# The order of four long neighbour lists, and a group that begins with its first two tiles

## The chip, the cores and the metric

The kernel runs on one core of a Trainium2 chip. The metric is the device time of one execution in microseconds (us). It is given as the median of three executions. Engines are called as in the profile: PE is TensorE, DVE is VectorE, ACT is ScalarE, POOL is GpSimd, SP is SyncE.

## What is computed

Sixteen graphs of 1024 nodes with 64 channels go through two layers. The second layer is the costly one. For every node it takes the list of its neighbours, drops a few of them by rank (dilation), and aggregates each channel by three interpolated quantiles over what is left. The essential lines of the reference are:

```python
# layer 0
h = jnp.maximum(_layernorm(x, axis=-1), 0.0)
x = x + matmul(adj / clip(sum(adj, axis=2), 1.0, None), h)
# layer 1
h = jnp.maximum(_layernorm(x, axis=-1), 0.0)
nb = (adj_ > 0) & (~eye)[None]
m = nb.sum(-1); rank = jnp.cumsum(nb, axis=-1) - 1
skip = jnp.where(m > 10, (m + 1) // 2, 1)
removed = nb & (skip > 1) & mask & ((rank + 1) % skip == 0)
rem = removed | swapaxes(removed, 1, 2)
adj_d = jnp.where(rem, 0.0, adj_)
agg = sum of wt * quantile(h of the neighbours in adj_d, tau) for tau in 0.25, 0.5, 0.75
x = x + (relu((h + agg) @ W1 + b1) @ W2 + b2) * mask
```

The adjacency is sparse and uneven: the first nodes of each graph have many neighbours, the later ones few. So most nodes have a short list, and a few have a long one.

## The kernel before, in words

The work has two stages, each of which is an ordered stream of instructions that a planner writes out while the kernel is built.

In the **first stage** (the pool `lay0`, line 1328) the batches are loaded one after another. Layer 0 is computed with transposes and products on PE. Each node's neighbours are listed as sorted keys with `max` operations on DVE. Every node's record (channels, the result of layer 0, 32 keys, its number and its mask) is scattered by POOL to `srt`, sorted by length of list. Four batches form a group, so there are four groups, and each has a table `tab` in DRAM with the rows that neighbours are gathered from. After a group is complete, its short lists are worked off; those of the groups 0 to 2 lie mostly within this stage. The last group (number 3) and the long lists come in the **second stage** (the pool `long`, line 1337).

`group` (line 1102) begins a group. It loads the records of all 32 tiles of 128 nodes (`recs`, one DMA of 544 KB). It then computes node numbers, gathers the full adjacency rows of the first tile (`gat_rows`), counts the neighbours of all tiles, and sorts the keys of tiles 1 to 31 (`keys`, with `max`, and `match_replace` where a list is longer than eight). It works out which neighbours are removed, in tile 1 from its keys and in tile 0 from the full row. It writes two dropped numbers per node into the table (`tab<-drop`, POOL), and copies the table to `whole` (SP). Then it adds one `Job` for each class of equal length.

`long_lists` (line 1239) treats the first tile's nodes of all groups together: four tiles of 128 nodes with at most 88, 31, 24 and 20 neighbours (`LONG`, line 40). For each list it loads the records (`lS`), gathers the adjacency rows (`lat`), finds the largest keys by segments, and makes the indices `lidx`. Then it adds a `Job` whose gathers write `lplaces0` (list 88, one buffer) or `lplaces` (the others, two buffers).

A `Job` (line 831) gathers one row per neighbour with one POOL instruction each (`run`, line 840). When all have landed, it marks removed neighbours (`rem`, `gone`, `ok`, `valid`, `q`, `wu` on DVE). ACT adds the marks to each gathered row. A sorting network of min and max on DVE follows, between `places` and `other` for short lists and between `lplaces` and `long_other` for long ones; there is one `long_other` and one set of `lgone` and `lwu`. ACT then scales the rows with the weights `w` or `lw` (128x67 for list 88), PE sums them with an identity matrix, and a small MLP (`layers`, line 1039) with ACT and PE follows. DVE adds the residual into `y`, and POOL scatters `y` to the output (`out_dram<-y`). `y` has six buffers.

The order of all instructions on an engine is fixed when the kernel is built, by the class `Plan` (line 234). Every stream names the engine of its next step and the earliest time for it. `Plan.run` (line 323) takes the step with the earliest time; among equal times the lower rank goes first. `Plan.note` (line 271) holds the cost model for each operation. The chip's engines then run their instructions strictly in that order, each waiting on semaphores for what it needs. The ranks that matter here are: -2000 for a group, -1500 for the preparation of long lists, -600 plus the number of the list for gathers of long lists, 100 times the group plus the class for short lists, 400 plus the number for the rest of long lists. DVE steps of a job get 900 less while fewer than 16 gathers are outstanding (`AHEAD`, line 214) and 2000 more otherwise. Outputs and MLP steps of short lists get -1000 and 5000 in the same two cases.

Nearly all instructions carry line 228, that of the helper which records them for the planner, so the profile is read by tile names.

Of the kernel before, what the change touches and what calls it, by code (L numbers as in the profile page):

```python
# [18 lines left out]
P = 128  # L19
# [9 lines left out]
NSEG = 4  # L29
# [204 lines left out]
class Plan:  # L234
# [4 lines left out]
    def __init__(self, nc):  # L239
        names = {"vector": "DVE", "scalar": "ACT", "tensor": "PE", "gpsimd": "POOL", "sync": "SP"}  # L240
        self.nc = SimpleNamespace(
            **{attr: Timed(self, name, getattr(nc, attr)) for attr, name in names.items()}
        )
        self.clock = dict.fromkeys([*names.values(), "DMA"], 0.0)
        self.ready, self.used, self.users = {}, {}, {}
        self.slots, self.streams = {}, []
        self.last = self.own = None
        self.parts = set()

    def tile(self, pool, shape, dtype, name, bufs, users=0):  # L250

# [16 lines left out]
    def at(self, *tiles):  # L268
        return max(self.ready.get(t.tensor.name, INF) for t in tiles)

    def note(self, engine, op, args, kwargs):
# [22 lines left out]
        elif engine == "PE":  # L294
            time = 0.1 + math.prod(out.shape[1:]) * 0.88e-3
            if op == "matmul" and rest[0].dtype == F32:
                time *= 2
        elif engine == "POOL":
            time, after = (1.27, 2.2) if op == "indirect_dma_start" else (0.15, 0.1)
            self.last = None  # L300
        else:
            start = max(start, self.clock["DMA"])
            busy = math.prod(out.shape) * 4 / 165e3

            time, after = 0.05, 2.2 + busy * (1 if 4 * out.shape[-1] >= 512 else 2)
            self.clock["DMA"] = start + busy
# [67 lines left out]
def list_path(ctx, tc, x, adj, nodemask, w1, b1, w2, b2, out, go):  # L374
# [727 lines left out]
    def group(g, kept=grp, name=""):  # L1102
# [16 lines left out]
        lists = recs[:, :, :8 * NSEG]  # L1119
        node = recs[:, :, REC - 2]  # L1120
        mask = recs[:, :, REC - 1]
        nodes = new(grp, [P, NTAU], F32, "nodes", 1)
        nc.vector.tensor_scalar(
            nodes, node, noff[:, s:s + 1], float(FIRST[g] * N), op0=OP.add, op1=OP.add
        )
        nodes_i = new(kept, [P, NTAU], I32, name + "nodes_i", 1 if name else 2)
        nc.vector.tensor_copy(nodes_i, nodes)
        progress["begun"] = g + 1
        yield "POOL", lambda: at(nodes_i)
        full = new(grp, [P, N], F32, "gat_rows", 1)  # L1130
        gather(full, adj_rows, nodes_i[:, 0:1])
        yield "DVE", always

        found = new(grp, [P, N], BF, "gfound", 1)[:, :NTAU * 8 * NSEG]
        found = found.rearrange("p (t e) -> p t e", t=NTAU)
        nc.vector.tensor_scalar(found, lists, 0.0, None, op0=OP.is_gt)
        m = tiny.tile([P, NTAU], F32, name="gm")
        nc.vector.tensor_reduce(m, found, AX.X, OP.add)
        over = tiny.tile([P, NTAU], F32, name="over")
        nc.vector.tensor_reduce(  # L1140
            over, found.rearrange("p t (s e) -> p t s e", e=8)[:, :, :, 7], AX.X, OP.max
        )
        nc.vector.memset(over[0 if four else HP:, 0:1], 0.0)
        big = tiny.tile([P, NTAU], F32, name="big")
        nc.vector.tensor_tensor(big, m, caps_sb, OP.is_gt)
        nc.vector.tensor_tensor(over, over, big, OP.max)
        nc.vector.tensor_reduce(ovf[:, g:g + 1], over, AX.X, OP.max)
# [5 lines left out]
        nc.vector.tensor_scalar(based, base, float(N), None, op0=OP.add)  # L1153

        drop = new(tiny, [P, 2, 2], F32, "drop", 2)
# [3 lines left out]
        for t in range(begin, NTAU):  # L1159
            nc.vector.max(out=keys[:, t, :8], in_=lists[:, t, :])  # L1160
            if caps[t] > 8:
                nc.vector.match_replace(
                    out=left, in_to_replace=keys[:, t, :8], in_values=lists[:, t, :],
                    imm_value=0.0,
                )
                nc.vector.max(out=keys[:, t, 8:], in_=left)
            if t % 8 == 0:
                yield "DVE", always

        assert all(cap <= T_THRESH for cap in caps[begin + 1:])  # L1170
        fst = slice(begin, begin + 1)
        skip = dilation(m[:, fst], mask[:, fst], 1)
        hit = tiny.tile([P, 2, 16], F32, name="hit")
        for e in range(2):
            nc.vector.tensor_scalar(
                hit[:, e, :], place1[:, :16], skip[:, e, :], None, op0=OP.is_equal
            )
            nc.vector.tensor_tensor(hit[:, e, :], hit[:, e, :], keys[:, begin, :], OP.mult)
        if four:
            nc.vector.tensor_reduce(drop[:, 1, :], hit, AX.X, OP.add)  # L1180
            nc.vector.tensor_scalar(
                drop[:, 1, :], drop[:, 1, :], -1.0, float(N), op0=OP.mult, op1=OP.add
            )
        for e in range(2):
            nc.vector.tensor_tensor(
                keys[:, begin, :], keys[:, begin, :], hit[:, e, :], OP.subtract
            )
        didx = new(tiny, [P, 2], I32, "didx", 2)
        index_of(didx, node[:, 0:2], float(PW), basep)
        idx = new(kept, [P, NTAU, 16], I32, name + "idx", 1 if name else 2)  # L1190
        index_of(idx, keys, -1.0, based)

        yield "DVE", lambda: at(full)
        nc.vector.scalar_tensor_tensor(
# [6 lines left out]
        skip = dilation(cum[:, N - 1:N], mask[:, 0:1], 1)  # L1201
# [6 lines left out]
        for e in range(2 if four else 1):  # L1208
# [8 lines left out]
                tc.declare_no_dep(ins.ins, other, reason="rows of their own")  # L1217
            other = ins.ins
        dropped = at(table)
        yield "SP", lambda: dropped  # L1220
        nc.sync.dma_start(whole[FIRST[g] * TS:R * TS, :], table)
        classes = []
# [16 lines left out]
    def long_lists(pool):  # L1239
# [1 line left out]
        yield "DVE", always  # L1241
        rev = new(pool, [P, N], HF, "rev", 1)
        nc.vector.tensor_scalar(rev, col_f, -1.0, float(N), op0=OP.mult, op1=OP.add)
        for l, K in enumerate(LONG):
            n = K + 1
            yield "SP", always
            S = new(pool, [P, 1, RW], F32, "lS", 4)
# [62 lines left out]
            for e in range(2):  # L1310
# [17 lines left out]
    with tc.tile_pool(name="lay0", bufs=2) as pool:  # L1328

        for stream, first in (  # L1330
# [303 lines left out]
```

## Time and profile before

| | us |
|---|---|
| median of three executions | 1513.86 |
| lowest, highest | 1511.95, 1516.6 |
| the profiled execution | 1512.82 |
| its span, first to last instruction | 1511.0 |

| engine | busy us | share of the span |
|---|---|---|
| DVE | 1191.3 | 79% |
| POOL | 957.2 | 63% |
| ACT | 816.4 | 54% |
| PE | 738.8 | 49% |

The span is divided by the stages at about 890 us. Before that point DVE is busy for 727 us of 890, and after it for 464 us. DMA moves 133 MB over the span, 88 GB/s on the mean; the two busy queues take 20.8% and 11.2% of the 16 engines' time.

A row of the timeline gives start, duration, engine, line, operation, output and inputs, and in brackets how long the engine had been idle and what ended that. A row of waits gives who waited for whom, total us, number of times and the longest. A row of busy times by stretch gives start and end, length, then busy us and count of instructions for PE, PE weight loads, DVE, ACT and POOL, then the granted PE clock, the busy share of the DMA engines and GB/s.

### The profile page before, as it was taken

How to read it: one execution, taken by the hardware profiler on the slowest of the kernel's cores; microseconds unless marked ns; L12 is line 12 of the kernel's file. 1: busy time of each engine (PE TensorE's matmuls, PEld its weight loads, DVE VectorE, ACT ScalarE, POOL GpSimd, SP SyncE). 2: the span in 40 equal slices, each digit the busy share in tenths (PEclk: the TensorE clock that was granted, in tenths of full speed). 3: DMA queues.
4: the chain of work that ended last, by engine and by line, in shares of the span. 5: the costliest groups of instructions: out<-in, count | busy, mean ns of one | idle time of the engine just before them, and what ended most of it. 6: DMA issues, size and time to landing. Idle time of an engine off the chain costs nothing. (4 is left out here: it accounts for less than half of the span.)

```text
span 1511.0 us, 15983 instructions
## 1 busy us (share of the span) xinstructions
PE 738.8 (49%) x3192; PEld 464.7 (31%) x3192; DVE 1191.3 (79%) x4104; ACT 816.4 (54%) x2789; POOL 957.2 (63%) x1154
## 2 busy tenths in 40 slices
PE   4778777327877556567667620024000123228542
PEld 2434334214544233343444320012000122216432
DVE  6777798997899779859869869893059999986875
ACT  7989878557879457757975520201050223148341
POOL 0122227777678757757777787667777777765083
PEclk8889888658888777869688755555555565558765
DMA  5445665424355253355341242111111111211010
GB/s 177 150 142 168 163 210 160 123 73 114 101 162 152 59 174 94 99 126 161 94 140 31 60 101 68 50 37 28 30 26 23 28 28 40 44 33 22 2 25 13
DMA packets 135718, 133.36 MB, mean 88 GB/s; under 512 B 100756, under 2 KB 103444, under 8 KB 135492
## 3 DMA queue, kind: packets, MB, share of 16 engines
q1 hardware_dynamic: 102876, 90.79, 20.8%
q0 software_dynamic: 32736, 41.47, 11.2%
q14 instruction: 78, 0.64, 0.1%
q8 instruction: 28, 0.46, 0.1%
HBM read 112.90 MB, written 23.61 MB: 90 GB/s over the span
## 5 line engine op out<-in xcount | busy, mean ns | idle before, releaser
L228 POOL DMA_INDIRECT places<-tab,idx x372 | 370.2, 995 | 131.7 <-issue 101.8
L228 PE MATMUL pt<-ident,prod 128*128 128x128 f32 (+1 forms) x736 | 160.2, 377 | 517.8 <-DVE prod L228 241.2
L228 PEld LDWEIGHTS pt<-ident,prod 128*128 128x128 f32 (+1 forms) x736 | 129.3, 256 | 550.4 <-ACT prod L228 412.4
L228 PE MATMUL ps_small<-att,h 128*65 128x512 f32 x512 | 254.7, 644 | 27.3 <-ACT h L228 10.5
L228 POOL DMA_INDIRECT srt<-row,to x128 | 125.9, 984 | 165.8 <-ACT row L228 144.0
L228 PE MATMUL pt<-ident,at 128*128 128x128 f32 x1024 | 176.7, 320 | 96.0 <-ACT att L228 71.1
L228 POOL DMA_INDIRECT lplaces<-whole,lidx x163 | 167.2, 1026 | 55.6 <-issue 48.5
L228 DVE MAX8 rec<-sg 128x8 f16<-128x256 f16 x512 | 180.1, 414 | 4.4
L228 PEld LDWEIGHTS pt<-ident,at 128*128 128x128 f32 x1024 | 136.9, 164 | 143.5 <-ACT att L228 93.8
L228 ACT ACTIVATE sg<-at 128x1024 f16<-128x1024 f32 x128 | 134.8, 1054 | 75.0 <-DMA at<-in_adj_dram 65.7
L228 ACT COPY att<-pt 128x512 f32<-128x512 f32 x256 | 141.9, 582 | 20.7 <-PE pt L228 18.8
L228 POOL DMA_INDIRECT places<-tab,last_idx x124 | 123.8, 998 | 41.3 <-issue 35.0
L228 PEld LDWEIGHTS ps_small<-att,h 128*65 128x65 f32 x512 | 74.7, 151 | 161.9 <-issue 123.2
L228 ACT ACTIVATE places<-places,gone 128x64 f32<-128x64 f32 x496 | 123.5, 335 | 0.5
L228 ACT ACTIVATE prod<-places,w 128x64 f32<-128x64 f32 x213 | 54.1, 336 | 120.5 <-DVE w L228 120.5
L228 POOL DMA_INDIRECT out_dram<-y,nodes_i x93 | 91.8, 987 | 22.6 <-issue 15.1
L228 DVE TENSOR_TENSOR sg<-sg,keyed 128x1024 f16<-128x1024 f16 x128 | 87.2, 681 | 23.7 <-ACT sg L228 23.7
L228 ACT ACTIVATE gone<-gone 128x15 f32<-128x15 f32 (+9 forms) x40 | 8.2, 206 | 169.2 <-DVE ok L228 169.0
L228 DVE TENSOR_TENSOR long_other<-lplaces 128x512 f32<-128x512 f32 (+5 forms) x124 | 64.1, 555 | 29.1 <-ACT lplaces L228 28.9
L228 DVE TENSOR_TENSOR other<-places,other 128x64 f32<-128x64 f32 (+6 forms) x204 | 69.6, 341 | 5.9
L228 PE MATMUL ps_small<-ot,w_sb 128*128 128x128 f32 (+3 forms) x112 | 47.6, 513 | 44.2 <-DVE y L228 31.2
L228 DVE TENSOR_TENSOR places<-places,other 128x64 f32<-128x64 f32 (+2 forms) x208 | 62.3, 309 | 4.9
(231 smaller groups left out, 1670.8 us busy)
## 6 DMA issues: line engine op xcount, KB each, us to landing
at<-in_adj_dram SPq DMA_DIRECT2D x128, 512.0 KB
places<-tab,idx POOLq DMA_INDIRECT x372, 2.5
whole<-tab SPq DMA_DIRECT2D x4, 1057.0 KB
tab<-row SPq DMA_DIRECT2D x16, 264.0 KB
xt<-in_x_dram SPq DMA_DIRECT2D x16, 256.0 KB
lplaces<-whole,lidx POOLq DMA_INDIRECT x163, 2.4
srt<-row,to POOLq DMA_INDIRECT x128, 2.7
places<-tab,last_idx POOLq DMA_INDIRECT x124, 2.4
```

Source lines behind the costliest of these rows:

```text
L228: ins = getattr(self._engine, op)(*args, **kwargs)
```

## The change

Three things change.

The long lists are prepared, gathered and ranked in the order 31, 24, 88, 20 instead of 88, 31, 24, 20. Buffers, capacities and the place of each list's nodes stay with the list.

A group loads the records of its first two tiles apart (`ahead`), ahead of the load of all records, which stays. From `ahead` it makes the row numbers of tile 0 (`row0`), gathers the adjacency rows, sorts the keys of tile 1, and computes and scatters the dropped nodes of both tiles. Only then does it wait for `recs`, sort the keys of tiles 2 to 31, make the indices, node numbers and counts, and copy the table. Each tile's keys 8 to 15 are set to zero one by one where the list is not longer than eight, instead of one memset of all keys.

In the second stage the planner takes PE's operations to be 1.5 times as long as before (`pace`). In the first stage it keeps 1.0.

```diff
+        self.pace = 1.0
...
+            time *= self.pace
...
+        ahead = new(kept, [P, 2, REC], F32, name + "ahead", 1 if name else 2)
+        nc.sync.dma_start(ahead, tiles[:, :2, R0:])
         nc.sync.dma_start(recs, tiles[:, :, R0:])
-        yield "DVE", lambda: at(recs)
+        yield "DVE", lambda: at(ahead) + 1.0
+        node = ahead[:, :, REC - 2]
+        nodes = new(grp, [P, NTAU], F32, "nodes", 1)
+        row0 = new(tiny, [P, 1], I32, "row0", 2)
+        index_of(row0, node[:, 0:1], 1.0, noff[:, s:s + 1])
+        if FIRST[g]:
+            nc.vector.tensor_scalar(row0, row0, FIRST[g] * N, None, op0=OP.add)
+        progress["begun"] = g + 1
+        yield "POOL", lambda: at(row0)
+        full = new(grp, [P, N], F32, "gat_rows", 1)
+        gather(full, adj_rows, row0)
+        yield "DVE", always
...
+        index_of(didx, node, float(PW), basep)
...
+        def first_keys(t, row):
+            nc.vector.max(out=keys[:, t, :8], in_=row)
+            if caps[t] > 8:
+                nc.vector.match_replace(
+                    out=left, in_to_replace=keys[:, t, :8], in_values=row, imm_value=0.0
+                )
+                nc.vector.max(out=keys[:, t, 8:], in_=left)
+            else:
+                nc.vector.memset(keys[:, t, 8:], 0.0)
...
+        first_keys(1, ahead[:, 1, :8 * NSEG])
+        m1 = tiny.tile([P, 1], F32, name="m1")
+        nc.vector.tensor_scalar(
+            left, ahead[:, 1, :8 * NSEG], 0.0, None, op0=OP.is_gt, op1=OP.add, accum_out=m1
+        )
+        skip = dilation(m1, ahead[:, 1, REC - 1:], 1)
...
+        yield "DVE", lambda: at(full)
...
+        skip = dilation(cum[:, N - 1:N], ahead[:, 0, REC - 1:], 1)
...
+        yield "POOL", lambda: at(drop)
...
+        dropped = at(table)
+
+        yield "DVE", lambda: at(recs) + 1.0
...
+        for t in range(2, NTAU):
+            first_keys(t, lists[:, t, :])
...
+        index_of(idx, keys, -1.0, based)
...
-        nc.vector.memset(keys, 0.0)
...
-        for l, K in enumerate(LONG):
+        for nth, l in enumerate((1, 2, 0, 3)):
+            K = LONG[l]
...
-                *(("lplaces", 2) if l else ("lplaces0", 1)), -600 + l, begin=at(whole),
-            )
-            plan.add(job.run(), 100 * NG + l)
+                *(("lplaces", 2) if l else ("lplaces0", 1)), -600 + nth, begin=at(whole),
+            )
+            plan.add(job.run(), 100 * NG + nth)
...
+    plan.pace = 1.5
     with tc.tile_pool(name="long", bufs=1) as pool:
```

More of the change, by code (lines that the diff above doesn't have):

```diff
@@ L1116, in group @@
         tiles = srt[g].rearrange("(t p) w -> p t w", p=P)
+        ahead = new(kept, [P, 2, REC], F32, name + "ahead", 1 if name else 2)
+        nc.sync.dma_start(ahead, tiles[:, :2, R0:])
         nc.sync.dma_start(recs, tiles[:, :, R0:])
-        yield "DVE", lambda: at(recs)
-        lists = recs[:, :, :8 * NSEG]
-        node = recs[:, :, REC - 2]
-        mask = recs[:, :, REC - 1]
+        yield "DVE", lambda: at(ahead) + 1.0
+        node = ahead[:, :, REC - 2]
         nodes = new(grp, [P, NTAU], F32, "nodes", 1)
-        nc.vector.tensor_scalar(
-            nodes, node, noff[:, s:s + 1], float(FIRST[g] * N), op0=OP.add, op1=OP.add
-        )
-        nodes_i = new(kept, [P, NTAU], I32, name + "nodes_i", 1 if name else 2)
-        nc.vector.tensor_copy(nodes_i, nodes)
+        row0 = new(tiny, [P, 1], I32, "row0", 2)
+        index_of(row0, node[:, 0:1], 1.0, noff[:, s:s + 1])
+        if FIRST[g]:
+            nc.vector.tensor_scalar(row0, row0, FIRST[g] * N, None, op0=OP.add)
         progress["begun"] = g + 1
-        yield "POOL", lambda: at(nodes_i)
+        yield "POOL", lambda: at(row0)
         full = new(grp, [P, N], F32, "gat_rows", 1)
-        gather(full, adj_rows, nodes_i[:, 0:1])
+        gather(full, adj_rows, row0)
         yield "DVE", always
[L1134 to L1147, printed above, removed]
         base = toff[:, s:s + 1]
@@ L1153, in group @@
         nc.vector.tensor_scalar(based, base, float(N), None, op0=OP.add)
+        didx = new(tiny, [P, 2], I32, "didx", 2)
+        index_of(didx, node, float(PW), basep)
         drop = new(tiny, [P, 2, 2], F32, "drop", 2)
         keys = new(kept, [P, NTAU, 16], F32, name + "keys", 1 if name else 2)
-        nc.vector.memset(keys, 0.0)
         left = tiny.tile([P, 8 * NSEG], F32, name="left")
-        for t in range(begin, NTAU):
-            nc.vector.max(out=keys[:, t, :8], in_=lists[:, t, :])
+        def first_keys(t, row):
+            nc.vector.max(out=keys[:, t, :8], in_=row)
             if caps[t] > 8:
                 nc.vector.match_replace(
-                    out=left, in_to_replace=keys[:, t, :8], in_values=lists[:, t, :],
-                    imm_value=0.0,
+                    out=left, in_to_replace=keys[:, t, :8], in_values=row, imm_value=0.0
                 )
                 nc.vector.max(out=keys[:, t, 8:], in_=left)
[L1167 to L1172, printed above, removed]
+            else:
+                nc.vector.memset(keys[:, t, 8:], 0.0)
+        assert begin == 1 and all(cap <= T_THRESH for cap in caps[2:])
+        first_keys(1, ahead[:, 1, :8 * NSEG])
[4 more added lines that the diff above has]
+        skip = dilation(m1, ahead[:, 1, REC - 1:], 1)
         hit = tiny.tile([P, 2, 16], F32, name="hit")
@@ L1177, in group @@
             )
[L1178 to L1191, printed above, removed]
+            nc.vector.tensor_tensor(hit[:, e, :], hit[:, e, :], keys[:, 1, :], OP.mult)
+        nc.vector.tensor_reduce(drop[:, 1, :], hit, AX.X, OP.add)
+        nc.vector.tensor_scalar(
+            drop[:, 1, :], drop[:, 1, :], -1.0, float(N), op0=OP.mult, op1=OP.add
+        )
         yield "DVE", lambda: at(full)
@@ L1200, in group @@
         nc.vector.tensor_tensor_scan(cum, nb, zeros, 0.0, op0=OP.add, op1=OP.add)
-        skip = dilation(cum[:, N - 1:N], mask[:, 0:1], 1)
+        skip = dilation(cum[:, N - 1:N], ahead[:, 0, REC - 1:], 1)
         for e in range(2):
@@ L1219, in group @@
         dropped = at(table)
+        yield "DVE", lambda: at(recs) + 1.0
+        lists = recs[:, :, :8 * NSEG]
+        node = recs[:, :, REC - 2]
+        mask = recs[:, :, REC - 1]
+        for t in range(2, NTAU):
+            first_keys(t, lists[:, t, :])
+            if t % 8 == 0:
+                yield "DVE", always
+        for e in range(2):
+            nc.vector.tensor_tensor(keys[:, 1, :], keys[:, 1, :], hit[:, e, :], OP.subtract)
+        nc.vector.memset(keys[:, 0, :], 0.0)
+        idx = new(kept, [P, NTAU, 16], I32, name + "idx", 1 if name else 2)
+        index_of(idx, keys, -1.0, based)
+        nc.vector.tensor_scalar(
+            nodes, node, noff[:, s:s + 1], float(FIRST[g] * N), op0=OP.add, op1=OP.add
+        )
+        nodes_i = new(kept, [P, NTAU], I32, name + "nodes_i", 1 if name else 2)
+        nc.vector.tensor_copy(nodes_i, nodes)
+        found = new(grp, [P, N], BF, "gfound", 1)[:, :NTAU * 8 * NSEG]
+        found = found.rearrange("p (t e) -> p t e", t=NTAU)
+        nc.vector.tensor_scalar(found, lists, 0.0, None, op0=OP.is_gt)
+        m = tiny.tile([P, NTAU], F32, name="gm")
+        nc.vector.tensor_reduce(m, found, AX.X, OP.add)
+        over = tiny.tile([P, NTAU], F32, name="over")
+        nc.vector.tensor_reduce(
+            over, found.rearrange("p t (s e) -> p t s e", e=8)[:, :, :, 7], AX.X, OP.max
+        )
+        nc.vector.memset(over[:, 0:1], 0.0)
+        big = tiny.tile([P, NTAU], F32, name="big")
+        nc.vector.tensor_tensor(big, m, caps_sb, OP.is_gt)
+        nc.vector.tensor_tensor(over, over, big, OP.max)
+        nc.vector.tensor_reduce(ovf[:, g:g + 1], over, AX.X, OP.max)
         yield "SP", lambda: dropped
```

## The prediction

> **What bounds the kernel now.** I began with the forty slices of the page, to find the stages:
>
> ```profile
> DVE  6777798997899779859869869893059999986875
> ...
> POOL 0122227777678757757777787667777777765083
> PEclk8889888658888777869688755555555565558765
> ```
>
> A slice is 37.8 us. Up to about 890 us (the 23rd or 24th digit) all engines work on batches. After that comes the stage that the change is about, the last group and the four long lists: POOL stays at 7 and DVE falls to 3 and 0 in slices 28 and 29, near 1060 to 1133 us. A gather holds POOL 0.94 us and is followed by 0.30 us of issue, so 7 tenths is a full POOL. Next I asked whom DVE waited for from 885 us on, since only that stage matters here:
>
> ```profile
> DVE lrem L228 <- DMA lplaces<-whole,lidx: 50.1, 2, 48.9
> DVE long_other L228 <- ACT lplaces L228: 28.9, 9, 5.7
> DVE y L228 <- PE ps_small L228: 28.1, 4, 14.1
> DVE other L228 <- ACT places L228: 13.6, 3, 11.2
> DVE nodes L228 <- DMA last_recs<-srt: 4.5, 1, 4.5
> ```
>
> One wait of 48.9 us stands out: the first step on a long list waits for its gathers. The timeline says why:
>
> ```profile
> 953.76 0.94 POOL L228 DMA_INDIRECT lplaces<-whole,lidx  x1 [0.30 <-issue]
> ...
> 1064.87 0.99 POOL L228 DMA_INDIRECT out_dram<-y,nodes_i  x1 [0.30 <-issue]
> ...
> 1096.53 0.34 DVE L228 TENSOR_TENSOR lrem<-lplaces,lS 128x176 f32<-128x176 f32 x1 [48.89 <-DMA lplaces<-whole,lidx]
> ...
> 1097.78 21.10 ACT L228 ACTIVATE lplaces<-lplaces,lgone 128x64 f32<-128x64 f32 x88
> ```
>
> List 88 goes first. Its 88 gathers, 14 output scatters in their midst and three POOL waits for `lnodes_i` take from 953.8 to 1094 us; then ACT adds the removed marks row by row for 21.1 us. The network runs at full speed only from 1118 us. Busy times by stretch (columns PE, PEld, DVE, ACT, POOL):
>
> ```profile
> 1040.00:1118.00 78.00, 7.12 (x30) 4.47 (x28) 6.43 (x19) 22.61 (x90) 60.58 (x76) 0.52 0.12 29
> 1118.00:1350.00 232.00, 44.08 (x190) 35.48 (x191) 223.81 (x725) 49.20 (x193) 178.50 (x180) 0.54 0.16 33
> 1350.00:1394.00 44.00, 32.46 (x202) 26.06 (x202) 23.79 (x67) 39.01 (x162) 27.02 (x35) 0.76 0.10 22
> 1394.00:1511.00 117.00, 48.66 (x280) 39.21 (x279) 83.96 (x303) 36.74 (x142) 44.03 (x60) 0.68 0.05 13
> ```
>
> So DVE idles 71.6 us in a **hole** before list 88, then is the bound for 232 us at 96%, idles 20.2 us while list 88 is scaled and summed, and at the end works through lists 31, 24 and 20 one after the other with 33 us idle. Those three networks come last although 31 and 24 had their gathers by 1172 us. The end is set by DVE work left behind the hole, not by POOL: its last short gather issues at 1382 us.
>
> **What the Trainium skill says.** "DMA: Bandwidth & Descriptors", Anatomy of one DMA, puts a gather at a fixed 2.0 us plus its bytes; the trace agrees for long lists (2.3 to 2.9 us to landing), while a gather of whole adjacency rows took 6.9 us. "SBUF — State Buffer", Who interferes with whom, says that a VectorE instruction with two SBUF inputs contends with a GpSimd instruction that reads SBUF. The trace fits in part: gathers took 0.94 us in the hole and often 1.38 us between 1122 and 1170 us, beside networks of two-input operations. "TensorE: Matmul & The Clock Gate", Part 1, says that an idle TensorE falls to half clock; the page shows PEclk 5 here, so PE steps after a pause are slow. "VectorE: DVE Perf Modes", The TRN2 errata, says that each VectorE instruction carries a fixed latency; 128x1 operations take 0.15 us here. I count small steps by number for that reason.
>
> **The change, part by part.**
>
> *Order 31, 24, 88, 20.* Nothing is added or removed; each list keeps its gathers, buffers and network. What moves is this:
>
> 1. Start of long gathers. The preparation of list 88 takes DVE from 916.3 to 952 us (36 us), that of list 31 from 957.1 to 977 us (20 us). With 31 first its indices stand 16 us earlier, but POOL was busy with group 2's gathers until 951 us. I take a start at 944 (954 if POOL is not free sooner), plus 4 for what happens before 890 us (below): 948.
> 2. List 88 then needs 31 + 24 + 88 = 143 gathers at 1.25 us (179), three row gathers (4) and the 14 scatters (14 x 1.27 = 18; 0 if they fall elsewhere). The POOL waits (1.5 + 4.5 + 3.9 us on `lnodes_i`) go, since a list is always queued. 948 + 201 = 1149, landed at 1151, 21 us of ACT: full speed at **1172** instead of 1118, 54 us later.
> 3. Filling the hole. The network of 31 ran from 1394 to 1426 (31.4 us of DVE, 32.5 with its seven opening steps), that of 24 from 1437 to 1462 (23.5, with them 25). 31 is gathered about 990 us, 24 about 1020; DVE frees at 1031. Even with 12 us between them for the single `long_other` buffer, both end by about 1115, before 1149. So 57.5 us of DVE work leaves the stretch behind the hole.
> 4. What is left behind 1172: 223.8 + 23.8 + 84.0 = 331.6, less 57.5: 274 us. Full speed to last work without idling: 1446.
> 5. Idle inside: the 232 us stretch idled 8; keep it. The pauses for 31 to 24 and 24 to 20 (6 us idle each) move into the hole or go. A new one appears: 20 waits for `long_other` until 88 is scaled, 67 rows (`lw` is 128x67) x 0.245 = 16.4 us of ACT, and its own 20 rows of marks, 4.9 us. Of these 21 us short jobs still in work hide some (before, 23.8 of 44 us). I take 10, bounds 0 and 21. The final scaling, summing, MLP and output after the last network stay as they are, 18 us idle, 2 us elsewhere.
> 6. List 20's 20 gathers, now behind 88's, were in the last stretch at 1434 to 1461 us under a busy DVE, because both `lplaces` buffers were held. They now put the short gathers back by 25 us, which about meets the saved waits: the last short gather stays near 1380. DVE still has some 60 us to do then, so this costs nothing; if DVE were ahead, it would cost up to 25.
>
> *Slower PE in the plan (1.5).* It adds no instruction; it moves results that DVE reads from PE later in its queue. DVE waited 28.1 us for such results after 885 us, 14.1 of them in the hole. I take 4 saved, bounds 0 and 10.
>
> *Group begun with two tiles.* SP gets one more DMA per group (128 x 2 records of 136 bytes, a sixteenth of the 544 KB), ahead of the records on SP's queue; it took 0.36 us there to issue those, and the loads behind it come that much later, hidden under 9.8 us of `lS` loads. In the last group DVE waited 4.5 us for all records; about 2 remain. Per group, one 0.48 us memset of all keys goes, 29 memsets of 8 columns at 0.06 us (1.7 us) and some eight 0.15 us steps (1.2 us) come: +2.4. There is also a lost cover: `gat_rows` was issued at 194.6 and read at 204.7 us, with 10 us of keys and counts between. Now only some 4 us of tile 1's steps lie there before the landing at about 8 us, so DVE may wait up to 4 us per group unless another stream's steps were planned in. Behind that wait stand the batches' steps on DVE. In return first gathers start some 5 us sooner, and at the first group POOL sat idle for 16.3 + 17.3 us. Three groups lie before 890 us, where DVE is 82% busy: +4, from -6 to +16. The early drop scatter and copy to `whole` (before, 923.8 and 927.2) are hidden; the indices of list 31 end later.
>
> *Sum.* 1172 + 274 + 8 + 10 + 18 + 2 - 4 = 1480 us of span against 1511.0. The profiled run took 1512.82, 1.8 more than its span; the median of three is 1513.86, 1.0 above that. Forecast for the median: **1483 us**, -2.0%.
>
> **Rivals.**
>
> *A fuller recovery, 1452.* The scatters fall outside the chain of gathers (-18) and short jobs cover 88's pause (-10), and a few us more from PE waits (-3). For it: short jobs have priority only while under 16 gathers are outstanding, so scatters can come between lists. Against it: they are held for output buffers that block short jobs.
>
> *Given back, 1515.* The network of 24 comes behind 88, as `long_other` is single and DVE keeps its written order: 25 us and 6 of pause return to the tail, 1483 + 31. Against it: 34 us of slack in step 3.
>
> *Slower, 1550.* DVE works strictly in the order written. If the plan puts the wait for 88's gathers ahead of the networks of 31 and 24, the hole grows by 54 us and nothing is taken out of the tail: 1513.9 + 54, less 18 of scatters that can no longer lie in the chain. It decides from the point where less than some 26 us of the 57.5 is done before 88's start (57.5 less the 31 us gained). Against it: the wait of 48.9 us shows that the plan lets gathers be late, not that other work was at hand.
>
> *The early start of a group costs more than it gives*, with the 16 us bound: 1495, inside the forecast's own band (1465 to 1498).
>
> **How the numbers follow.** The forecast has 0.56, the fuller recovery 0.18, given back 0.15 (half within 0.3%, the rest split), slower 0.11. A measurement here tells about 0.3% (4.5 us) from no change. Faster 0.56 + 0.18 + 0.04 = 0.78, same 0.08, slower 0.14. The range runs from 1447 to 1510: its low end is the fuller recovery with a start at the low bounds (-5), and above it lie the upper half of given back and the slower case, 0.19 together.
>
> **What would show it.** `lrem` of a 31-row list near 1000 us, networks of 31 and 24 done before 1149, list 88's marks at about 1151, DVE near 96% from 1172 to about 1440, then one pause and list 20 alone in the tail. DVE waits on `gat_rows` in each group would show the lost cover. It is wrong if `lrem` of list 88 is the first long step again, if POOL pauses between lists, or if the pause before list 20 exceeds 21 us.

## The result, and the profile after

| | before | after |
|---|---|---|
| median of four executions, us (lowest to highest) | 1512.9 (1508.1 to 1516.6) | 1550.41 (1546.6 to 1553.82) |
| span of the profiled execution, us | 1511.0 | 1549.6 |
| first stage: up to the load of the last group's records | 890.8 | 951.9 |
| second stage: from there to the end | 620.2 | 597.7 |

The ratio is 1.0237, with a 95% interval from 1.0214 to 1.0261. The forecast was 1483 us, range 1447 to 1510: the kernel became slower where I had put 0.78 on faster. One row of the table says where. The second stage, which the change is about, got 22.5 us shorter. The first stage, for which I had put 4 us, got 61 us longer.

The forty slices of the changed kernel, now 38.7 us each:

```profile
DVE  6878689987667788777889847899970199999944
...
POOL 0222257775735857766778777776777787577522
PEclk9889885676977858777966675555655555555576
```

The hole of VectorE (0 and 1) has moved from slices 28 and 29 to 31 and 32, and behind it DVE is full up to the last two slices instead of the 8, 6, 8, 7, 5 of before. That is what the change was to do. But slices 7 to 24, the first stage from the work on the first group on, hold three 9s instead of seven. The boundary of the stages is the time at which SP issues the load of the last group's records ("890.8 to 890.8" below is its first and last start). Before:

```profile
L228 SPq DMA_DIRECT2D last_recs<-srt x1: 360/360/360, 890.8 to 890.8; - x1
```

After, with the new load of two tiles just ahead of it:

```profile
L228 SPq DMA_DIRECT2D last_ahead<-srt x1: 360/360/360, 951.9 to 951.9; - x1
L228 SPq DMA_DIRECT2D last_recs<-srt x1: 467/467/467, 952.3 to 952.3; - x1
```

**The second stage after.** The first steps on the four long lists, from the timeline:

```profile
1065.52 0.21 DVE L228 TENSOR_TENSOR lrem<-lplaces,lS 128x62 f32<-128x62 f32 x1
...
1126.58 0.20 DVE L228 TENSOR_TENSOR lrem<-lplaces,lS 128x48 f32<-128x48 f32 x1
...
1215.07 0.35 DVE L228 TENSOR_TENSOR lrem<-lplaces,lS 128x176 f32<-128x176 f32 x1 [43.40 <-DMA lplaces<-whole,lidx]
```

Lists 31 and 24 are worked off ahead of list 88, as forecast. Whom DVE waited for in this stage:

```profile
DVE lrem L228 <- DMA lplaces<-whole,lidx: 43.4, 1, 43.4
DVE long_other L228 <- ACT lplaces L228: 32.4, 9, 9.9
DVE y L228 <- PE ps_small L228: 28.3, 5, 9.8
DVE lat L228 <- DMA lat<-in_adj_dram,lnodes_i: 4.0, 3, 1.6
DVE gat_rows L228 <- DMA gat_rows<-in_adj_dram,row: 1.6, 1, 1.6
```

The wait for list 88 is hardly shorter than the 48.9 us of before: two networks were put ahead of it, and it moved back by about as much. What is gained is that the networks no longer stand at the end. Busy times by stretch (columns as in the prediction):

```profile
951.90:1215.00 263.10, 67.05 (x280) 50.23 (x279) 188.67 (x692) 55.35 (x214) 193.09 (x198) 0.55 0.19 43
1215.00:1236.00 21.00, 0.00 (x0) 0.00 (x0) 4.64 (x13) 19.95 (x84) 16.05 (x17) 0.50 0.13 28
1236.00:1549.60 313.60, 105.62 (x482) 82.05 (x482) 262.45 (x860) 93.12 (x363) 186.75 (x216) 0.57 0.11 25
```

**The first stage.** From the first group's records to the last group's, before and then after:

```profile
180.00:890.80 710.80, 453.47 (x1896) 275.58 (x1896) 593.42 (x2078) 493.56 (x1661) 502.35 (x623) 0.76 0.43 118
```

```profile
178.80:951.90 773.10, 474.56 (x1917) 282.79 (x1915) 604.32 (x2196) 496.70 (x1663) 523.20 (x648) 0.73 0.40 110
```

The stretch is 62.3 us longer, DVE is busy for only 10.9 us more, and idles 168.8 us instead of 117.4. Of the 10.9, some 8 are steps of short lists that came earlier (DVE is busy 8.0 us less in the second stage; over the whole span it has 2.7 us more). So 51 of the 62 us are idle time. The loads of the four groups came at 178.8, 451.1, 711.2 and 951.9 us; before, they came at 180.6, 412.7, 656.8 and 890.8. So 38 of the 61 us were there when the second group was loaded. Whom it waited for in that stretch, before:

```profile
DVE other L228 <- ACT places L228: 18.0, 8, 4.8
DVE rem L228 <- DMA places<-tab,idx: 16.7, 7, 4.9
DVE sg L228 <- ACT sg L228: 13.4, 3, 8.7
DVE base L228 <- PE ps_small L228: 10.7, 3, 6.5
```

and after:

```profile
DVE other L228 <- ACT places L228: 36.0, 9, 5.9
DVE deg L228 <- PE ps_small L228: 28.5, 4, 11.7
DVE rem L228 <- DMA places<-tab,idx: 20.2, 7, 8.6
DVE ln_v L228 <- ACT ln_sq L228: 14.3, 8, 4.2
DVE base L228 <- PE ps_small L228: 12.1, 5, 5.1
...
DVE gat_rows L228 <- DMA gat_rows<-in_adj_dram,row: 3.5, 2, 2.3
```

None of the long waits is for anything that the change added. `deg` and `ln_v` belong to the batches, `other` to the networks of short lists. The one wait that I had feared, `gat_rows`, is 3.5 us in three groups.

**Theories.** A: the new beginning makes the planner write the whole first stage in another order, and this order leaves DVE waiting more. B: the steps, loads and waits of the new beginning cost the 61 us themselves. C: the order of the lists is what loses. In the experiments "the planner's clock" is the time that the program's own planner had reached on VectorE when the last batch was written. It comes from its cost model (`note`) while the kernel is built, not from a chip: 871 us for the kernel before, 912 us for the changed one.

### The profile page after: what moved, and what is told of

Same layout as the page of the kernel before. It is cut to its first block, busy times and chain, and to the rows that moved or that the text cites. A ratio compares the mean times of both kernels' runs of the same rounds, so it can differ in the third digit from the quotient of the medians.

```text
span 1549.6 us, 16092 instructions
## 1 busy us (share of the span) xinstructions
PE 775.4 (50%) x3192; PEld 483.2 (31%) x3192; DVE 1194.0 (77%) x4234; ACT 821.7 (53%) x2797; POOL 956.3 (62%) x1150
## 5 line engine op out<-in xcount | busy, mean ns | idle before, releaser
L228 PE MATMUL pt<-ident,prod 128*128 128x128 f32 (+1 forms) x736 | 167.6, 389 | 466.6 <-DVE prod L228 275.9
L228 PE MATMUL ps_small<-att,h 128*65 128x512 f32 x512 | 265.9, 668 | 52.5 <-DVE y L228 17.1
L228 PEld LDWEIGHTS pt<-ident,prod 128*128 128x128 f32 (+1 forms) x736 | 135.3, 268 | 501.0 <-ACT prod L228 239.8
L228 PE MATMUL pt<-ident,at 128*128 128x128 f32 x1024 | 181.7, 328 | 131.8 <-ACT att L228 115.8
L228 PEld LDWEIGHTS pt<-ident,at 128*128 128x128 f32 x1024 | 142.2, 169 | 180.1 <-ACT att L228 141.1
L228 POOL DMA_INDIRECT lplaces<-whole,lidx x163 | 161.4, 990 | 49.7 <-issue 48.5
L228 POOL DMA_INDIRECT out_dram<-y,nodes_i x93 | 96.8, 1041 | 25.2 <-issue 14.8
L228 DVE TENSOR_TENSOR long_other<-lplaces 128x512 f32<-128x512 f32 (+6 forms) x124 | 64.2, 554 | 32.9 <-ACT lplaces L228 32.4
L228 ACT COPY ot<-pt 128x128 f32<-128x128 f32 (+3 forms) x56 | 22.1, 397 | 106.8 <-PE pt L228 99.0
L228 DVE TENSOR_TENSOR other<-places,other 128x64 f32<-128x64 f32 (+6 forms) x204 | 69.6, 341 | 5.8
L228 POOL DMA_INDIRECT out_dram<-y,last_nodes_i x31 | 32.2, 1039 | 62.0 <-DVE y L228 56.1
```

Of the source, the lines that this page charges most:

```text
L228: ins = getattr(self._engine, op)(*args, **kwargs)
```

## The experiments

Eight kernels ran on two chips on which everything, the kernel before too, takes some 30% longer (1973.65 and 1991.12 us); of these only ratios and stages of the same chip are compared.

### e1_order, y4_order, z1_order: the list order alone

```
-        for l, K in enumerate(LONG):
+        for nth, l in enumerate((1, 2, 0, 3)):
+            K = LONG[l]
```

The ranks take `nth` in place of `l`.

> Only the order of the long lists is changed; group and planner are as before. Theory A (the loss comes from the first stage, whose written order changes with the group's new steps, and the order of the lists gains): the first stage ends at 890 us as before, the second is 20 to 35 us shorter, 1478 to 1494 us. Rival B (the order of the lists loses by itself, the hole before list 88 grows and nothing is filled): 1530 to 1550 us. Rival C (the order is worth nothing): within 5 us of 1513.

> The kernel before with the list order 31, 24, 88, 20 alone. The first stage is that of before, 891 us. My forecast's steps 1 to 5 without the rest of the change: 1490 us, ratio 0.985. Theory C (POOL gives all 163 long gathers precedence over the 49 short ones that group 2 still has to issue, so VectorE runs dry behind the networks of 31 and 24 and again behind the wait for list 88): two waits of 30 to 45 us as in the kernel with all three in the second stage, ratio 1.002 to 1.010.

> The list order alone once more, if possible on a chip like that of the forecast. My forecast's steps 1 to 5 without the rest: 1490 us, ratio 0.985. Theory C (the long gathers go ahead of the short ones that group 2 still has to issue, so that VectorE runs dry in front of list 88 a second time): 1518 to 1530 us, ratio 1.003 to 1.010, with the first stage at 891 us and one wait of 30 to 50 us in front of list 88.

Measured: 1.0082 (1.006 to 1.0103) and 1.0059 (1.002 to 1.0098) on the slow chips, and on an ordinary chip 1515.73 us against 1515.94: 0.9998 (0.9985 to 1.0011). Neither my gain of 1.5% nor theory C's loss there. Stages 892.5 and 619.6 us. The long wait that theory C named is there, but it only takes the place of the 48.9 us of before. Whom DVE waited for up to 1182 us:

```profile
DVE lrem L228 <- DMA lplaces<-whole,lidx: 45.6, 1, 45.6
DVE long_other L228 <- ACT lplaces L228: 25.0, 7, 8.1
DVE y L228 <- PE ps_small L228: 8.6, 1, 8.6
```

The stage, cut at 1182 us, where list 88's network gets to full speed:

```profile
892.50:1182.00 289.50, 50.83 (x221) 38.11 (x219) 188.96 (x653) 67.87 (x270) 213.81 (x223) 0.55 0.20 43
1182.00:1512.10 330.10, 118.86 (x564) 92.04 (x564) 272.33 (x898) 106.38 (x413) 206.10 (x235) 0.59 0.13 26
```

Behind that point DVE has 272 us to do, and I had worked out 274: the work left the tail. But the point comes 289.5 us after the records, not 277, and DVE then idles 57.8 us, not 38. The first of these differences, 12.5 us, is about what POOL waited for `lnodes_i`. My step 2 had let these waits go, and between 892 and 1182 us they are there:

```profile
POOL lat L228 <- DVE lnodes_i L228: 12.9, 2, 9.0
```

In the changed kernel POOL stands still for 3.9 and 7.7 us at the same steps. The list order alone gives back all that it takes. It doesn't explain a loss of 2.4% either.

### e3_group, z2_group: the new beginning alone

The function `group` of the changed kernel in the kernel before; lists in the old order, no `pace`.

> Only the group's new beginning, in all four groups; long lists 88, 31, 24, 20 and no factor. Theory A: the first stage ends about 950 us as in the changed kernel, and the second is as long as before or a few us shorter: 1562 to 1576 us, the slowest of the four. Rival B (the list order loses, not the group): within 15 us of 1513.

> The new beginning in all four groups, lists in the old order, no slower TensorE in the plan. Theory A: the first stage is written exactly as in the changed kernel, so the last group's records are loaded at 952 us again; behind it the old order of the lists. Ratio 1.015 to 1.03: all of the change's loss comes with this part. If the list order were the cause: 1.005 or below.

Measured: 1.0211 (1.0156 to 1.0267) on a slow chip; on an ordinary one 1575.84 us, 1.0399 (1.0355 to 1.0442), above the expected band. The load of the last group:

```profile
L228 SPq DMA_DIRECT2D last_ahead<-srt x1: 359/359/359, 952.9 to 952.9; - x1
```

The first stage is the changed kernel's within 1 us, and the second, 621.2 us, is the old one. So all of the loss comes with the new beginning, and behind this first stage the rest of the change wins back some 1.6%.

### x1_due: another order of the first stage, and no new beginning

```
-        yield "DVE", lambda: at(recs)
+        yield "DVE", lambda: at(recs) + 4.0
```

> The kernel before with one number changed: in the written order, the first VectorE step of each group may come 4 us after the landing of its records instead of at once. No instruction, transfer or buffer is added or taken away, only the order in which the program writes its instructions. Theory A (the loss is the order of the first stage, which any shift of a group's beginning deals anew): the planner's own clock puts the end of the first stage at 905 us instead of 871 us, so the records of the last group are loaded some 30 to 60 us later and the ratio is 1.02 to 1.03. Theory B (the loss is the cost of the instructions, the second gather of records and the waits that the new beginning adds): nothing of these is in here, ratio 1.000 within 0.3%.

Measured: 1551.63 us, 1.0212 (1.0182 to 1.0243). The planner's clock had moved by 34 us, the load of the last records moved by 37, to 928.0; the second stage is 622.2 us. DVE has 4103 instructions against 4104; ACT has 13 more of 2,800, since the planner also chooses which of the two adds the marks. Whom DVE waited for between 180 and 928 us:

```profile
DVE deg L228 <- PE ps_small L228: 27.5, 5, 9.2
DVE rem L228 <- DMA places<-tab,idx: 21.8, 5, 10.2
DVE other L228 <- ACT places L228: 21.6, 7, 5.6
DVE sg L228 <- ACT sg L228: 15.1, 6, 6.1
```

The wait for `deg`, which the kernel before doesn't have in this stretch, stands here too with 27.5 us, without any step of the change. The delay itself, if nothing hid it, would be 12 us in the three groups of this stage; the rest comes from the order. And the order doesn't move one way: the second group was loaded at 397.9 us, 15 us earlier than before, the third at 682.3, 25 us later. Theory A is shown to be enough for a loss of this kind: one due time of 4 us costs 37 us of first stage, where the change costs 61, and nearly as much in the ratio.

### x3_slack, y1_ahead3, z3_ahead3: the whole change, other numbers in the planner

```
-SLACK = 2.0
+SLACK = 3.0
```

> The whole change, with one constant of the planner changed: SLACK, the time that the plan leaves between a result of another engine and the step that reads it, is 3 us instead of 2. All instructions of the change stay. The planner's own clock puts the end of the first stage at 872 us instead of 912 us. Theory A: most of the first stage's loss goes, the records of the last group are loaded near 900 to 920 us instead of 952 us, and the ratio falls from 1.024 to between 0.99 and 1.01. Theory B: the added instructions and waits are all still there, ratio 1.02 or above.

For the other two, with `SLACK` at 2:

```
-        yield "DVE", lambda: at(ahead) + 1.0
+        yield "DVE", lambda: at(ahead) + 3.0
```

> The whole change with one number altered: the first VectorE step on the two tiles may come 3 us after their landing in the plan instead of 1. No instruction is added or removed, and no other constant touched. The planner's own clock puts the end of the first stage at 886 us instead of 912. Theory A (the order dealt to the first stage decides): by the four kernels known so far the chip comes 20 to 40 us after the planner's clock, so the last group's records are loaded at 906 to 926 us instead of 952, and the ratio falls to 1.00 to 1.015. Theory B (the instructions and waits of the new beginning decide): 952 us and 1.024 again.

> The whole change with the first VectorE step on the two tiles due 3 us after their landing in the plan instead of 1. Theory A (the order decides): last group's records at 906 to 926 us, ratio 1.00 to 1.012. Theory B (the steps and waits decide): 952 us, ratio 1.024.

Measured: x3_slack 1536.52 us, 1.0104 (1.0071 to 1.0137), just above its band of 0.99 to 1.01, stages 903.8 and 632.6 us. y1_ahead3, on a slow chip, 1.0102 (1.0056 to 1.0148). z3_ahead3 1541.09 us, 1.0143 (1.0101 to 1.0184), a little above its band; its profiled execution, with a span of 1549.3 us the longest of five, has stages of 925.4 and 623.9 us. All steps of the new beginning are still there, and 48 and 27 us of the 61 are gone from the first stage. Theory B can't explain that. `z3_ahead3` is the cleaner of the two, since `SLACK` moves other steps too and was not tried on the kernel before. In these profiles both kernels give most of it back in the second stage, 35 of the 48 us and 26 of the 27.

| kernel | planner's clock, us | on the chip, us | difference |
|---|---|---|---|
| before | 870.7 | 890.8 | 20.1 |
| x1_due | 905.0 | 928.0 | 23.0 |
| x3_slack | 872.2 | 903.8 | 31.6 |
| z3_ahead3 | 885.7 | 925.4 | 39.7 |
| after | 911.8 | 951.9 | 40.1 |

The chip follows the planner, but kernels with the new beginning come 9 to 20 us later against it than the two without. (The first stages of z2 and z5 have the same planner's clock as the changed kernel's, and ended at 952.9 and 955.9 us: 4 us are chance.) So of the 61 us some 41 are the order as the planner itself sees it, with the few added steps in it. Up to 20 are something that it doesn't price, and most of that stays open. The waits for `gat_rows` (3.5 us) lie in it: the planner counts on a gather's rows 2.2 us after its 1.27 us on POOL, and the first row gather was read 5.5 us after its issue.

### x4_added: work on VectorE, with the old order

```
...
+        for _ in range(60):
+            tc.nc.vector.memset(spare, 0.0)
+        for _ in range(16):
+            tc.nc.vector.tensor_scalar(spare1, spare, 1.0, None, op0=OP.add)
```

> The kernel before with 60 small memsets (128x8) and 16 small additions put on VectorE in each of the four groups, behind the issue of the row gather, without the planner knowing of them, so that the written order of everything else is the old one. That is about twice what the new beginning adds in instructions. Theory A: they fill idle time or cost their own 5 to 7 us per group at most, ratio 1.000 to 1.012. Theory B: twice the direct cost of the change, ratio 1.03 or above.

Measured: 1556.55 us, 1.0253 (1.0225 to 1.028), outside theory A's band and short of theory B's. My "about twice" was right for the number of instructions only:

```profile
L1136 DVE MEMSET spare<- x240: 65/65/65, 193.6 to 935.8; 128x8 f32 x120
L1138 DVE TENSOR_SCALAR spare<-spare x64: 170/172/395, 201.6 to 939.5; 128x8 f32<-128x8 f32 x64
```

240 x 0.065 + 64 x 0.172 is 26.6 us of DVE time. The change adds 2.7 us of busy time, since its 116 small memsets hide in the `max` steps between which they stand. At the first group 29 of these `max` steps took 2.77 us before (from 199.02 us on); with a memset behind each they took 3.38 us after (from 204.85 us on). 26.6 us in one burst per group cost 39 us, 1.5 us each; at that rate, as an estimate, 2.7 us cost 4. The run says that the start of a group is dear, and that the change adds too little there to explain 61 us.

### e2_order_pace, e4_last, x2_last, y2_last_old, z4_last_old: parts of the second stage

e2 is e1 with the slower TensorE of the plan:

```
+            time *= self.pace
...
+    plan.pace = 1.5
```

> The order of the long lists and the factor 1.5 on PE in the planner's second stage; group as before. Theory A: like the order alone, less 0 to 10 us: 1474 to 1490 us, the first stage unchanged. Rival B: 1530 us or more. If the factor reshuffles the second stage badly: slower than the order alone by 5 us or more.

e4 and x2 are the same kernel: e2 with the new beginning for the last group alone (the old function stays for the first three):

```
-        plan.add(group(NG - 1, pool, "last_"), -2000)
+        plan.add(group_ahead(NG - 1, pool, "last_"), -2000)
```

> Order of the lists, factor 1.5, and the group's new beginning in the last group alone, which lies in the second stage. Theory A: the first stage is as before, 890 us, and the second as in the changed kernel, 598 us: 1488 to 1492 us. If the new beginning costs in the last group too, it is slower than the order with the factor; if it helps, up to 10 us faster. Rival B: 1530 us or more.

> The changed kernel with the new beginning in the last group only; the first three groups begin as before, so the first stage has the old order to the last instruction. Theory A: the second stage keeps what it won (597.7 us of the changed kernel's profile against 620.2 us), the first stage stays at its 891 us, so 1485 to 1495 us, ratio 0.982 to 0.989. Theory C (the order of the lists itself loses): ratio 1.00 or above. If the chip is a slow one again, the earlier ratio of 0.994 should come back.

y2 and z4 have this last edit alone:

> The kernel before with the new beginning in the last group alone: lists in the old order, no slower TensorE in the plan. The first stage is that of before, 891 us. Theory A (in the second stage the new order of the lists loses what the early beginning wins): ratio 0.985 to 0.995, below the 1.0033 of the kernel that has all three in the second stage. Theory C (the early beginning of the last group costs time): 1.003 or above.

> The new beginning in the last group alone, lists in the old order. First stage 891 us. Theory A (the early beginning wins a little, the order of the lists loses it): ratio 0.990 to 1.000, below that of the list order alone. Theory D (nothing in the second stage wins, each new order there is a draw about the old one): 1.000 to 1.008, as on the slower chip.

Measured: e2 1.0045 (1.0027 to 1.0063), e4 0.9939 (0.9917 to 0.9961), x2 on an ordinary chip 1.0033 (1.0019 to 1.0046), with stages of 895.1 and 625.0 us. The gains that I had expected of e1, e2, e4 and x2 (0.982 to 0.989 for x2) all failed to come. y2 1.0049 (1.0008 to 1.009), above the 0.985 to 0.995 of its theory A; z4 0.9983 (0.9969 to 0.9997), within its theory A, stages 896.4 and 616.1. With the old first stage, no combination of the parts moved the time by more than 1%, and the sign changes from chip to chip. With the early beginning of the last group alone, z4's second stage is 4 us shorter than before and its first 5.6 longer; the ratio is 2.6 us below 1 there and 10 above it in y2, so neither sign is settled. In x2 DVE stood still twice around list 88:

```profile
1155.61 0.34 DVE L228 TENSOR_TENSOR lrem<-lplaces,lS 128x176 f32<-128x176 f32 x1 [45.22 <-DMA lplaces<-whole,lidx]
1190.10 0.20 DVE L228 TENSOR_TENSOR rem<-places,recs 128x36 f32<-128x36 f32 x1 [32.71 <-DMA places<-tab,idx]
```

The second is a short list of group 2 whose gathers POOL issued behind the long ones, and list 88's network stands behind it in the queue. z1 has only the first of the two, and its stage is 619.6 us against 625.0.

### y3_late12: another draw for the kernel before

```
-LATE = 14.0
+LATE = 12.0
```

> The kernel before with one constant of the planner changed, LATE 12 us instead of 14 (how long after TensorE's result the final additions and output scatters are due). No instruction changes. The planner's own clock puts the end of the first stage at 851 us instead of 871. Theory A: the order of the first stage is a draw that any number in the planner deals anew, here a good one: last records at 870 to 890 us, ratio 0.985 to 1.000. If the planner's clock says nothing of the chip: anything from 880 to 950 us.

Measured, on a slow chip: 1.0181 (1.0143 to 1.0218), a miss: the planner's clock promised 20 us, but the last records came at 1180.3 us there, as in the two kernels with the old order on that chip (1179.9 and 1180.9), and the second stage took 842.6 us against their 824.6 and 814.9. The planner's clock ranks orders only roughly.

### z5_group_order, z6_fewer: why the order wins only behind the long first stage

z5 is the change without `pace`:

> The whole change without the slower TensorE in the plan: new beginning in all groups and list order 31, 24, 88, 20. The first stage is that of the changed kernel, 952 us, with 28 short gathers left behind it. If those 21 fewer gathers let the order win: second stage 595 to 605 us, ratio 1.022 to 1.030. If the slower TensorE in the plan makes the win: second stage 615 to 625 us, ratio 1.036 to 1.042.

z6 is z1 without 21 output scatters, whose rows stay unwritten:

```
+        if others is scatters and 84 < count[0] <= 105:
...
+            return
```

> The list order alone, with 21 of the output scatters left out: those that POOL issued between the last long gather (1197 us) and the last short one (1418 us), so 21 x 128 rows of the output are not written. The planner still counts them, so every other instruction stands in its old order. VectorE's work is the same; POOL has 21 x 1.27 = 27 us less, as much as 21 gathers. Theory POOL (POOL's chain of gathers and scatters has become the bound of the second stage): last short gather near 1391 us instead of 1418, second stage 595 to 605 us instead of 619.6, ratio 0.984 to 0.991. Theory VectorE (its work behind the hole still sets the end): the gathers come earlier and nothing else does, 615 to 620 us, ratio 0.997 to 1.000.

Measured: z5 1543.38 us, 1.0172 (1.0139 to 1.0205), below both of its bands, with stages of 955.9 and 588.7. Against z2 the list order takes 32.5 us out of the second stage. z6 1514.03 us, 0.9985 (0.9972 to 0.9999): theory VectorE. The last short gather came at 1399.0 us instead of 1418.2, and the rest as before:

```profile
892.20:1182.00 289.80, 52.71 (x230) 40.02 (x229) 188.44 (x652) 66.47 (x264) 213.83 (x224) 0.55 0.20 43
1182.00:1420.00 238.00, 59.48 (x234) 44.27 (x234) 228.64 (x739) 62.11 (x241) 159.77 (x158) 0.54 0.16 30
1420.00:1511.60 91.60, 59.18 (x330) 47.53 (x330) 43.74 (x160) 45.57 (x179) 24.56 (x45) 0.70 0.03 10
```

POOL is 22 us less busy, DVE's columns are those of z1, and the end is the same. So POOL time behind list 88's gathers isn't the bound, and my "not by POOL" holds there. The second stage of z5:

```profile
955.90:1189.00 233.10, 56.95 (x242) 42.13 (x241) 185.37 (x675) 50.44 (x196) 171.76 (x176) 0.55 0.21 45
1189.00:1231.90 42.90, 0.00 (x0) 0.00 (x0) 4.71 (x13) 20.05 (x84) 32.50 (x43) 0.50 0.13 28
1231.90:1544.60 312.70, 112.52 (x520) 87.85 (x520) 265.94 (x877) 98.18 (x381) 191.81 (x212) 0.59 0.13 26
```

Full speed comes 276 us after the load (z1: 289.5), 265.9 us of DVE work follow (272.3), and 46.8 us of idle time (57.8). Together 31 us.

## Why the prediction was wrong

The step that failed is **"Group begun with two tiles"**: "Three groups lie before 890 us, where DVE is 82% busy: +4, from -6 to +16." I counted its instructions, its load and its lost cover, and these I had, if anything, too dear: the lost cover cost 3.5 us in the three groups instead of up to 12, the added DVE work 2.7 us in all instead of 2.4 per group. The first group's short gathers did begin sooner, 30.6 us after its load instead of 36.3. What I didn't count is that a `yield` in `group` is an input of a greedy planner. Each due time in it decides what all engines do next, from 190 us to the end. I had written that the order is fixed when the kernel is built and had still priced the part as if everything around it stayed in place. The order after it was another draw: +41 us by the planner's clock, +61 on the chip. x1_due shows that a due time alone can do this (37 us), x3_slack and z3_ahead3 that 48 and 27 us of it go while all steps stay, z2_group that the whole loss lies here.

The other steps, each measured from the load of the last group's records, which my sum had at 894.8 us (890.8 and 4):

| step | forecast | after | z5: without pace | z1: order alone |
|---|---|---|---|---|
| 1: first long gather | 53 | 49 | 47 | 53 |
| 2: full speed of list 88 | 277 | 284 | 276 | 290 |
| 4: DVE work behind it | 274 | 262 | 266 | 272 |
| 5: idle behind it | 38 | 51 | 47 | 58 |
| second stage | 589 | 598 | 589 | 620 |

(The forecast column leaves out the 4 us for the slower TensorE of the plan; with it, 585.)

- Steps 1, 3 and 4 held: the networks of 31 and 24 went ahead of list 88, and 59 to 69 us of DVE work left the tail (331.6 before, 272.3 in z1, 266 and 262 in the others).
- Step 2 held within 7 us in z5 and in the changed kernel. In z1 list 88 came 13 us late, about as much as POOL's waits for `lnodes_i`, which did not go; in z5, which has 10.5 us of them, the long gathers began 6 us sooner. The waits stood in the midst of the lists, behind 13 and 33 of the long gathers, where the row gathers of the next lists were queued. No sign of being wrong that I had named looked at the length of the first stage.
- Step 5: the pauses behind list 88 were larger than 38 us in all three. In the changed kernel DVE waits 9.9 us near the end for the last of list 88's scaling and list 20's marks, which is the pause that I had put at 10, and 9.8 us for `ps_small` just before, which I had not named.
- Step 6 fell where the order stood alone. In z1 the last short gather issued at 1418.2 us and not near 1380. But that cost nothing as far as z6 shows, where it came 19 us sooner and the end stayed.
- "Slower PE in the plan": -4 forecast, +9 found in the second stage (597.7 against 588.7; ratios 1.0237 against 1.0172). On a slow chip e2 was 0.4% below e1. The sign isn't settled.
- Sum: 1549.6 - 1480 is 69.6 us: 57 from the first stage (61.1 less 4), 13 from `pace` (9 and 4), nothing from the rest. That split takes z5's second stage as given, and z5's match is in part luck: 1 us and 8 us less in steps 2 and 4, 9 us more in step 5.
- The second stage came as forecast only behind the long first stage. Where the first stage kept its old order, the second took 620 us (z1) and 625 us (x2), and the kernels took 1516 and 1522 us. So by these two runs 1483 would have been missed even with my +4 for the first stage come true, by steps 2 and 5: 277 and 38 us forecast, 290 and 58 in z1.

The slower rival named 1550 us, and the time came out there, but by another mechanism: it had list 88's wait ahead of the networks of 31 and 24, and they went first. Nothing is to be learned from the match.

**Open.** Why the list order gains 32 us behind the long first stage and nothing behind the old one. Other runs exclude three answers: that only the early beginning of the last group was missing (x2 has it and gains nothing), that 21 fewer short gathers help by themselves (z2 has 28 left like z5, and takes 621.2 us with the old order), and POOL's load behind list 88 (z6). The runs show a pattern, though. The table has, for the kernels on ordinary chips (x4 and z6 apart, which add or leave out work), how many short gathers of the groups before the last POOL had still to issue at the boundary, and how long the second stage took:

| list order | kernels | short gathers left | second stage, us |
|---|---|---|---|
| old | before, z4, x1, z2 | 49, 49, 32, 28 | 620, 616, 622, 621 |
| new | z1, x2, x3, z3 | 49, 49, 51, 47 | 620, 625, 633, 624 |
| new | after, z5 | 28, 28 | 598, 589 |

The list order gained only where few short gathers were left, and they were few only where the first stage was long. x3 and z3 are the whole change, and with a shorter first stage their second stage gains nothing either: no kernel has both halves of the forecast. Whether the number left is the cause, or another trait of those orders, no run shows, since none changed it alone. Open too is the up to 20 us by which kernels with the new beginning fall behind the planner's clock.

## What to carry to other kernels

Where a greedy planner writes the order, the price of an edit isn't the price of its instructions: a change of a due time, or of another number of the planner, can deal the whole order behind it anew, here with 27 to 48 us up or down on a first stage of 891 (x1, z3, x3; nothing in the first stage of y3). The planner's clock is known as soon as the kernel is built, and 41 of the 61 us stood in it before any run. Before forecasting such an edit, look how far the time moves when a due time is shifted without touching a step, and put that spread into the range. And judge the parts of a change apart, each with the other parts' order as well as without it: the list order was worth 2% behind the long first stage and nothing behind the old one, so gains found in different kernels can't simply be added.

## What the runs showed of the hardware

Two of the chips that the runs used took 1974 and 1991 us for the kernel that takes 1513 to 1518 on the others, at a granted TensorE clock of about 0.64 instead of about 0.69 to 0.70. VectorE's busy time is the same on both kinds (1191.6 us in e1, 1188.5 in z1, one kernel), so what it took longer there it waited. The order of kernels was partly another (e4 0.9939, x2 1.0033 for the same kernel).

A gather of 128 full rows landed after different times: `lat` after 6.9 us in the profile before and after 4.8 us in the changed one, `gat_rows` there after 4.5 us (medians of four). The first `gat_rows`, issued at 189.54 us, was read at 195.05 after a wait of 2.28. I had put its landing at about 8 us, which is one reason why the lost cover was dear in the forecast.

A memset of 128x8 took 65 ns of VectorE's time where memsets stood in a row, and some 20 ns where each stood behind a `max` at the first group of the changed kernel (0.61 us for 29 of them, from the two times given with x4).
